# An adaLN transformer block in fp32: the down weights' sums moved to batch 0's projections, and work of gate/up pinned behind PE's reads

## The chip, the cores and the metric
The kernel runs on one core of a Trainium2 chip. The metric is the device time of one execution in microseconds (us). The kernel before took 2990.94 us in the median of 3 runs (2985.1 to 2992.16). One more execution was profiled; all durations below are from it.

Five engines work beside each other, each in its own order: TensorE (PE, matrix products), VectorE (DVE), ScalarE (ACT), GpSimd (POOL) and SyncE (SP), which here issues most DMAs. They meet through semaphores.

## The reference
Two batches of 1024 tokens with D = 1024, 32 heads, a hidden width of 2752 in the feed-forward part, all in fp32:

```python
mod = (_silu(c) @ wmod).reshape(2, 6, 1, -1)         # shifts, scales, gates
h = _layernorm(x) * (1 + ca) + sa
q, k, v = split(clip(h @ Wqkv.T, -8, 8)); q, k = LN(q), LN(k)
x = x + ga * (softmax(causal(q k^T * scale + alibi)) v) @ Wout.T
h = _layernorm(x) * (1 + cb) + sb
out = x + gb * ((silu(h @ Wg.T * ag) * (h @ Wu.T * au)) @ Wd.T * ad)
```

Wg, Wu and Wd are ternary (-1, 0, 1), which the kernel doesn't use.

## The kernel before
**Fast products.** Large products are done by the Strassen-Winograd scheme: a product of 2 x 2 blocks takes seven block products (P1, P2, U2, P5, U3, P53, U6) in place of eight, at the price of sums of blocks. A's operands are A11, A12, A22 and the sums S1 to S4, B's are B11, B21, B22 (B12 only enters sums) and T1 to T4. The gate, up and down products use the scheme twice, one inside the other: seven outer **stages** (`STAGES`), each with seven inner products (`CHAIN`). The outer sums of the weights and of the activations need memory and engines other than PE; much of the kernel's order is about where they go.

**Stages, in order of time.**
1. Modulation vectors, and batch 0's projections (`projections`, from about 47 to 400 us): parts 0, 1 and 2 (q, k, v) of four token pairs j each. Part and pair make a running number n = 4 * part + j. For parts 1 and 2 the operand a of a pair comes back from memory (L930, `a<-hop`); part 0 makes it from tokens. A part's weights wB are loaded by `weights_b` (L806), for batch 0 with sums on DVE and POOL (L814, L816). Between the seven products a list `Todo` of smaller PE work runs (transposes, modulation pieces wm with their own loads at L655). `extra(todo, n)` adds this work for number n. Four pieces of wm are held at a time, so a load waits until PE has used an older piece.
2. Attention over both batches, with batch 1's projections and the out projection woven in by a planner (`together`, `share`). Not touched.
3. The last token pairs: `second_batch` makes, from both batches' halves, the B operands of gate/up (outer sums T1 to T4, then inner sums by `inner_b`, L1161 to L1164, each four subtractions of 128x256 and stores to `bop_dram`). `second(j)` calls it for pair j; the last one, `second(3, nc.vector)`, stands right before gate/up and is all on DVE.
4. Gate/up: five slabs s of 512 hidden columns. For each slab four quarters of both weights are loaded (`gate_weights`), their outer sums made by `gate_sums` (L1615 to L1618, POOL, 128x1024 each), and then come 7 stages n_ with 7 steps each. A step multiplies one inner operand of gate and of up (`sig`, `siu`, or a block of the weights; inner sums at L1626 to L1629 on POOL) by one loaded operand `bt` of 512 KB (`moving`, L1638, six buffers, SP's queue). Each step has two groups of four matmuls, 1.72 us apart: 3.43 us. `merge` (L1565 to L1576) adds a finished bank to the partial results, on DVE or ACT. PE can't write a bank again before its merge has read it.
5. Within gate/up a queue holds side work with due times: `after(n, go)` puts it n steps ahead, and `run_due` emits it. In it are the Silu and the product by up (`final`, L1683 and L1684) and the outer sums of the activations, which are stored to `act_dram` (L1751, L1752). Stage A11 writes X, A12 writes C, S1 writes Z and so on; two more POOL sums stand after S2 and S3 (L1730, L1737).
6. Also within gate/up, one slice of the down weights per stage for the first 20 stages in program order: `down_load` (L1176, two loads of 256 KB, tile wdr), and five steps later `down_weights` (L1184 to L1187, four POOL subtractions of 128x256 into wdo; L1189, four stores of 128 KB to `wdop`).
7. Down: 7 stages of 4 pairs (`products`, L1843 the matmuls, `finish` the output). A stage's weights are loaded in four pieces (`stage_weights`, L1812), T1 to T4 of the inner scheme made at L1813 to L1816; the activations of a pair are one tile aq of 1280 KB (L1823, three buffers). The tiles dsi hold the activations' inner sums (`ais`, three buffers).

**What sets the order.** The program states the work in one order; a scheduler then orders each engine's instructions by priority and by its own idea of when they are ready, unless a dependency or a pin (`behind`, a dependency without a semaphore on the same engine) forbids it. On the chip each engine runs its list strictly in order. SP does the same with DMAs: a store whose source isn't ready holds every load behind it. A memory region is reused when a pool that lies over it is opened, so the first tile there waits for the last reads of the old one.

Of the kernel before, what the change touches and what calls it, by code (L numbers as in the profile page):

```python
# [480 lines left out]
def kernel(  # L481
# [376 lines left out]
    class Todo:  # L858
# [15 lines left out]
        def places(self, q0, n):  # L874

            order = [q for _, _, _, q in SEVEN]

            def between(q):
                if order.index(q) >= q0:
                    yield from self.run(n)  # L880

            return between
# [26 lines left out]
    def projections(b, pools, banks, places, extra=None, other=None):  # L909
# [7 lines left out]
        for part in range(3):  # L917
            bt = weights_b(wp_, wqkv_t[:, ts(part, D)], f"{b}_{part}", wt_dram[part], other, b == 0 and part == 1)
            for j in range(NT // 2):
# [19 lines left out]
                def read(q, bank):  # L939
# [13 lines left out]
                    lambda q, i: a[:, SLOT[q], i, :], bt, banks, read, todo.places(q0, n), KC // 2  # L953
# [202 lines left out]
    def inner_b(o, block, j, pool, eng):  # L1156

        v = block.rearrange("p (q c) h t -> p q c h t", q=2)
        b11, b12, b21, b22 = v[:, 0, :, 0], v[:, 0, :, 1], v[:, 1, :, 0], v[:, 1, :, 1]
        t_ = pool.tile([P, 4, 2, P], FP, tag="inner", name=f"inner_{o}_{j}", bufs=2)  # L1160
        eng.tensor_sub(t_[:, 0], b12, b11)  # L1161
# [6 lines left out]
        nc.sync.dma_start(to[:, 3:7, j], t_)  # L1168

    def down_load(i, pool):  # L1170

        s, c_ = i // 4, i % 4
        w = pool.tile([P, 4, 2, P], FP, tag="wdr", name=f"wdr_{i}")
        rows_ = wd_t[ds(s * 4 * P, 4 * P), :].rearrange("(j p) e -> p j e", p=P)
        for n in range(2):
            nc.sync.dma_start(w[:, :, n], rows_[:, :, ds(n * HALF + c_ * P, P)])  # L1176
        return w

    def down_weights(i, w, pool):

        s, c_ = i // 4, i % 4
        B11, B12, B21, B22 = (w[:, 2 * kh : 2 * kh + 2, n] for kh, n in ((0, 0), (0, 1), (1, 0), (1, 1)))
        ot = pool.tile([P, 4, 2, P], FP, tag="wdo", name=f"wdo_{i}")
        nc.gpsimd.tensor_sub(ot[:, 0], B12, B11)  # L1184
        nc.gpsimd.tensor_sub(ot[:, 1], B22, ot[:, 0])
        nc.gpsimd.tensor_sub(ot[:, 2], B22, B12)
        nc.gpsimd.tensor_sub(ot[:, 3], B21, ot[:, 1])  # L1187
        for r, o in enumerate(("T1", "T2", "T3", "T4")):
            nc.sync.dma_start(wd_dram[o][:, s, :, ts(c_, P)], ot[:, r])  # L1189
# [111 lines left out]
    def second_batch(j, pool, h0, h1, half):  # L1301
# [4 lines left out]
        nc.vector.tensor_sub(t1, lo1, t1)  # L1306
        nc.vector.tensor_sub(t2, hi1, t1)
        half.tensor_sub(t3, hi1, lo1)
        half.tensor_sub(t4, t4, t2)
        for o, v, eng in (  # L1310
            ("T2", t2, nc.vector), ("T1", t1, nc.vector), ("T3", t3, half),
            ("B22", hi1, nc.vector), ("T4", t4, half),
        ):
            inner_b(o, v, j, pool, eng)
# [73 lines left out]
    with ExitStack() as st:  # L1388
# [3 lines left out]
        wosp = st.enter_context(tc.tile_pool(name="wos", bufs=1))  # L1392
        nxp = st.enter_context(tc.tile_pool(name="next", bufs=1))
# [20 lines left out]

        def extra(todo, n):
# [6 lines left out]
            if n == 3:  # L1422
# [13 lines left out]
        dense0 = projections(0, qpools, banks, 2, extra, wxp)  # L1436
# [55 lines left out]
    opools, _, bt, todo, _ = out_args  # L1492
    rest_st = ctx.enter_context(ExitStack())
    rest_pool = right["rest"] = rest_st.enter_context(tc.tile_pool(name="rest", bufs=1, side="right"))
    rps = rest_st.enter_context(tc.tile_pool(name="rest_ps", bufs=4, space=PSUM))

    def fetch(b, j, eng=nc.sync):
        kept[b, j] = rest_pool.tile(
# [7 lines left out]
    def second(j, eng=nc.gpsimd):  # L1506
        second_batch(j, rest_pool, kept[0, j], kept[1, j], eng)
# [51 lines left out]

    def merge(q, bank, to, frm, part_t, pool, nm):  # L1560

        if q in ("P1", "U2", "P5"):
            m, n = {"P1": (0, 0), "U2": (0, 1), "P5": (1, 1)}[q]
            part_t[q] = pool.tile(list(bank.shape), FP, tag=f"{nm[0]}{q}", name=f"{nm}_{q}")
            if frm is None:  # L1565
                nc.scalar.copy(part_t[q], bank)
            else:
                nc.vector.tensor_add(part_t[q], frm(m, n), bank)  # L1568
            return
        m, n = QUAD[q]  # L1570
        if q != "U6":
            nc.vector.tensor_add(to(m, n), part_t[MATE[q]], bank)  # L1572
        elif frm is None:
            nc.scalar.copy(to(m, n), bank)
        else:
            nc.vector.tensor_add(to(m, n), frm(m, n), bank)  # L1576

    with ExitStack() as ff:
# [9 lines left out]
        with ExitStack() as gu:  # L1588
# [23 lines left out]
            def gate_sums(W):  # L1612
                for mat in ("g", "u"):
                    o = W[mat]
# [330 lines left out]
```

## Time and profile before

| | |
|---|---|
| median of 3 runs | 2990.94 us (2985.1 to 2992.16) |
| profiled execution: time, span | 2987.97 us, 2986.3 us |
| mean granted clock of PE | 0.965 |
| PE idle, 0 to 400 us | 36 us (363.90 busy) |
| 400 to 1570 (attention to gate/up's start) | 116 us (1053.90 busy) |
| 1570 to 1762 (gate/up, slab 0) | 42 us (149.87 busy) |
| 1762 to 2472 (gate/up, slabs 1 to 4) | 16 us (693.53 busy) |
| 2472 to 2986 (down) | 35 us (478.52 busy) |
| moved by DMA | 579.12 MB, mean 194 GB/s |

How to read it: the span runs from the first to the last instruction of the profiled execution, the time has a little around it. Busy times of engines overlap. A timeline line has the start, the time, the engine, the source line, the operation, what it writes and reads, and in brackets the idle time before it and what ended it. A line of the waits has the total, the number and the longest. PE's two stretches of waiting on a matmul group are seen against the groups beside them: a group of four 128x512 matmuls takes 1.88 us from first start to last end when PE runs at its full clock.

### The profile page before, as it was taken

To read this page: it belongs to the slowest core of one execution; us is meant where nothing else is said; L and a number is where in the kernel's file an instruction comes from. 1 tells how busy PE (TensorE), PEld (TensorE's weight loads), DVE (VectorE), ACT (ScalarE), POOL (GpSimd) and SP (SyncE) were. 2 spreads that over 40 slices of the span, in tenths; PEclk is the share of its full clock that TensorE was granted. 3 is DMA by queue.
4 is the path that set the end of the run, shared out by engine and by line. 5 is a ranking of instruction groups with operands and counts; after the bars stand their busy time and mean duration, and the time that the engine had idled before them with its cause. 6 is when DMAs were issued, how large, how long until landed. Compare 5 with 4: busy or idle time off the path is not lost. (4 is left out here: it accounts for less than half of the span.)

```text
span 2986.3 us, 29722 instructions
## 1 busy us (share of the span) xinstructions
PE 2739.7 (92%) x10271; PEld 1339.0 (45%) x10271; DVE 1476.0 (49%) x2295; ACT 687.2 (23%) x1523; POOL 1277.0 (43%) x1140
## 2 busy tenths in 40 slices
PE   7999899999998888888997869999999997999998
PEld 2444333333332222224563324444444446888776
DVE  5666424566453456564564333453535354444553
ACT  1322144444434455553111001010101100000000
POOL 3211033334354555564555556564635540222343
PEclk9999999999999899999998989999999998999999
DMA  9777762534535445334777778675766658555542
GB/s 347 278 269 290 273 210 98 186 136 162 182 109 187 140 152 156 115 113 131 226 247 227 240 246 276 187 276 169 270 183 229 197 176 258 159 143 141 152 141 79
DMA packets 376931, 579.12 MB, mean 194 GB/s; under 512 B 20950, under 2 KB 278072, under 8 KB 365636
## 3 DMA queue, kind: packets, MB, share of 16 engines
q1 hardware_dynamic: 366904, 559.78, 57.5%
q10 hardware_dynamic: 9868, 17.35, 1.8%
q8 instruction: 84, 1.38, 0.2%
q14 instruction: 75, 0.61, 0.1%
HBM read 411.89 MB, written 165.17 MB: 193 GB/s over the span
## 5 line engine op out<-in xcount | busy, mean ns | idle before, releaser
L1053 ACT ACTIVATE p<-sc,kw 128x128 f32<-128x128 f32 (+3 forms) x1024 | 422.1, 514 | 335.1 <-PE sc L745 320.2
L1085 POOL TENSOR_TENSOR p<-p,p 128x1024 f32<-128x1024 f32 (+3 forms) x128 | 265.3, 2072 | 255.8 <-PE av L745 227.1
L745 PE MATMUL bank<-wT,a 128*128 128x512 f32 x768 | 361.4, 613 | 13.6 <-DVE wT L814 6.8
L1085 DVE TENSOR_TENSOR p<-p,p 128x1024 f32<-128x1024 f32 (+3 forms) x192 | 248.8, 1309 | 118.1 <-POOL p L1057 69.7
L745 PE MATMUL bank<-wB,a 128*128 128x512 f32 x576 | 265.0, 604 | 2.7 <-DVE raw L947 2.2
L745 PE MATMUL sc<-cq,ck 32*128 32x512 f32 (+3 forms) x1536 | 198.3, 557 | 68.9 <-ACT p L1053 68.5
L1057 POOL TENSOR_SCALAR_AFFINE_SELECT p<-p 128x256 f32<-128x256 f32 x256 | 136.6, 544 | 227.3 <-ACT p L1053 224.4
L745 PEld LDWEIGHTS bank<-wT,a 128*128 128x128 f32 x768 | 141.8, 194 | 200.3 <-issue 177.2
L745 PE MATMUL av<-p,cv 128*32 128x512 f32 (+3 forms) x1536 | 170.5, 513 | 3.9 <-POOL p L1057 3.9
L745 PEld LDWEIGHTS bank<-wB,a 128*128 128x128 f32 x576 | 104.8, 191 | 148.1 <-issue 129.6
L1712 PE MATMUL gx<-bt,sig 128*128 128x512 f32 x280 | 135.4, 607 | 31.6 <-DVE g_P L1568 18.3
L1712 PE MATMUL gy<-bt,sig 128*128 128x512 f32 x280 | 135.3, 606 | 25.6 <-DVE gX L1572 20.6
L745 PEld LDWEIGHTS sc<-cq,ck 32*128 32x128 f32 x1536 | 66.2, 190 | 201.7 <-ACT p L1053 118.5
L1712 PE MATMUL ux<-bt,siu 128*128 128x512 f32 x280 | 134.6, 604 | 2.2 <-DVE u_U L1568 1.1
L1712 PE MATMUL uy<-bt,siu 128*128 128x512 f32 x280 | 132.3, 595 | 0.0
L949 DVE TENSOR_TENSOR raw<-P,bank 128x512 f32<-128x512 f32 x48 | 32.9, 686 | 159.8 <-PE bank L745 157.5
L1712 PEld LDWEIGHTS gx<-bt,sig 128*128 128x128 f32 x280 | 53.3, 192 | 101.4 <-issue 99.7
L1712 PEld LDWEIGHTS gy<-bt,sig 128*128 128x128 f32 x280 | 53.7, 194 | 95.4 <-issue 72.1
L745 PEld LDWEIGHTS av<-p,cv 128*32 128x32 f32 x1536 | 33.3, 110 | 120.9 <-issue 86.8
L1712 PEld LDWEIGHTS ux<-bt,siu 128*128 128x128 f32 x280 | 54.3, 195 | 73.7 <-issue 70.3
L1712 PEld LDWEIGHTS uy<-bt,siu 128*128 128x128 f32 x280 | 53.8, 192 | 68.3 <-issue 67.3
L1712 PE MATMUL gx<-bt,wgS 128*128 128x512 f32 x160 | 75.4, 593 | 2.1 <-DMA bt<-bop_B 1.1
(418 smaller groups left out, 4516.1 us busy)
## 6 DMA issues: line engine op xcount, KB each, us to landing
bt<-bop_T SPq DMA_DIRECT2D x140, 512.0 KB
bt<-bop_B SPq DMA_DIRECT2D x99, 512.0 KB
a<-hop SPq DMA_DIRECT2D x20, 1792.0 KB
wm<-in_L_wmod_dram SPq DMA_DIRECT2D x48, 512.0 KB
wB<-in_L_attn_Wqkv_dram SPq DMA_DIRECT2D x21, 1024.0 KB
aq_S<-act_S SPq DMA_DIRECT2D x16, 1280.0 KB
qk<-qs SPq DMA_DIRECT2D x16, 1024.0 KB
act_S<-asS SPq DMA_DIRECT2D x30, 512.0 KB
```

The source lines that it names most:

```text
L745: return in_order(nc.tensor.matmul(*args, **kw_))
L949: nc.vector.tensor_add(dst, part_t[MATE[q]], bank)
L1053: nc.scalar.activation(p[:, g, lo:hi], sp[:, g, lo:hi], AF.Exp, bias=kw[:, d, h_ : h_ + 1])
L1057: nc.gpsimd.affine_select(out=p[:, :, 0:P], in_=p[:, :, 0:P], pattern=[[0, 2], [1, P]], compare_op=ALU.is_ge, fill=0.0, base=0, channel_mu ...
L1085: adders[b](half, jb).tensor_add(dst, dst, ps[half][:, :, 0:n])
L1712: nc.tensor.matmul(ps.rearrange("p (j t) -> p j t", j=NJ), ins[mat][qa][:, c2, :], bt[:, :, c2, :], start=(q in ("P1", "P2", "P5") and c2 ...
```

## The change
It has five parts.

1. The 20 down-weight slices move from gate/up's stages to batch 0's projections. A function `side(n, e)` is called before each of the seven products e of number n; for n in 1, 2, 3, 5, 6, 7, 9 it emits one slice at each even e, three for each n and two for n = 9, so 9 slices in part 0, 9 in part 1 and 2 in part 2. A slice is now four loads of 128 KB into one tile of five parts, four POOL subtractions in place, four stores. The pool has two buffers. `mod_load` of the first wm pieces starts at n = 2 and not 3.
2. `second(3)` is no longer one block before gate/up: its two outer sums on DVE and the inner sums of T1, T2 and B22 are queued for the steps after 1 to 5, T3 and T4 on POOL for the steps after 8 to 11. The pools of results Z and of activation sums open two stages later, when the pair's pool is closed.
3. `gate_sums` is cut into quarters: 32 POOL operations of 128x256 a slab instead of 8 of 128x1024.
4. In `final` the Silus and the products by up are queued apart, the products one or two steps after the Silus. The activation sums have due times of their own, the last (S4) later than the others. What DVE runs from the queue is pinned: its first instruction stands `behind` the last merge emitted on DVE (`last_read`).
5. Down's pools are opened in another order, so that its weights and aq lie over the gate/up weights' regions; B12 has its place with the T tiles, B22 has one for even and one for odd stages, ais has two buffers instead of three. The first stage's weights and the first two aq are issued on ACT's queue (`nc.scalar`) and not SP's.

The core of the diff:

```diff
+        def side(n, e):
+            at = (1, 2, 3, 5, 6, 7, 9)
+            if n in at and e % 2 == 0 and at.index(n) * 3 + e // 2 < min(4 * NSB, at.index(n) * 3 + 3):
+                down_weights(at.index(n) * 3 + e // 2, dwp)
...
-            if n == 3:
+            if n == 2:
                 loaded.extend(mod_load(wmr, nc.sync, *pieces[i]) for i in range(AHEAD))
...
-        w = pool.tile([P, 4, 2, P], FP, tag="wdr", name=f"wdr_{i}")
+        w = pool.tile([P, 5, 2, P], FP, tag="wdr", name=f"wdr_{i}")
...
+        for kh in range(2):
+            for n in range(2):
+                nc.sync.dma_start(w[:, 2 * kh + n], rows_[:, 2 * kh : 2 * kh + 2, ds(n * HALF + c_ * P, P)])
+        nc.gpsimd.tensor_sub(w[:, 0], w[:, 1], w[:, 0])
+        nc.gpsimd.tensor_sub(w[:, 4], w[:, 3], w[:, 0])
+        nc.gpsimd.tensor_sub(w[:, 1], w[:, 3], w[:, 1])
+        nc.gpsimd.tensor_sub(w[:, 2], w[:, 2], w[:, 4])
+        for o, r in (("T1", 0), ("T2", 4), ("T3", 1), ("T4", 2)):
+            nc.sync.dma_start(wd_dram[o][:, s, :, ts(c_, P)], w[:, r])
...
-            second(3, nc.vector)
...
-                    nc.gpsimd.tensor_add(o["S1"], o["S3"], o["A22"])
...
+                    for k in range(4):
+                        o = {q: v[:, k] for q, v in W[mat].items()}
+                        nc.gpsimd.tensor_add(o["S1"], o["S3"], o["A22"])
...
             def run_due(all_=False):
                 while queue and (all_ or queue[0][0] <= count[0]):
-                    queue.pop(0)[1]()
+                    read = last_read[0]
+                    ins_ = queue.pop(0)[1]()
+                    if ins_ is not None and read is not None:
+                        behind(ins_, read)
+            on_dve, on_pool = second_batch(3, pair_pool, kept[0, 3], kept[1, 3])
+            for e, go in enumerate(on_dve):
+                after(1 + e, go)
+            for e, go in enumerate(on_pool):
+                after(8 + e, lambda go=go: (go(), None)[1])
...
+                    for l in range(2):
+                        after(n, lambda l=l: silu(l))
+                    for l in range(2):
+                        after(n + 1 + l, lambda l=l: product(l))
...
+                            n = 7 + 4 + l if e == 3 else z + 2 + (3 * l + e) // 2
+                            after(n, lambda r=r, l=l: go(*r, l))
...
-                    i = next(slices, None)
-                    if i is not None:
-                        wd_ = down_load(i, dwp)
-                        after(5, lambda i=i, wd_=wd_: down_weights(i, wd_, dwp))
...
+            wdp, aqp, wtp, aip, dpp, dxp, late, drp, fnp, dlp = (
+                dn.enter_context(tc.tile_pool(name=n, bufs=k))
+                for n, k in (
+                    ("wdq", 1), ("aq", 3), ("wdt", 1), ("ais", 2), ("dpart", 2), ("dresx", 1),
+                    ("wdl", 1), ("dres", 1), ("fin", 3), ("drest", 1),
+                )
+            )
...
-                nc.sync.dma_start(
+                (nc.sync if n_ or i > 1 else nc.scalar).dma_start(
                     aq, act_dram[oa][:, :, :, :, ts(i, P)].rearrange("p s l h t -> p (s l) h t")
...
-                wt = stage_weights(STAGES[n_][1])
+                wt = stage_weights(STAGES[n_][1], n_ % 2, nc.sync if n_ else nc.scalar)
```

## The prediction, made before the changed kernel was run
> **What bounds the kernel now.** I read the page's busy times first, then its chain of work that ended last, the waits of the whole core, the timelines of TensorE (PE), VectorE (DVE), GpSimd (POOL) and SyncE (SP) around each wait of PE, and last the windows of 50 us.
>
> ```profile
> PE 2739.7 (92%) x10271; PEld 1339.0 (45%) x10271; DVE 1476.0 (49%) x2295; ACT 687.2 (23%) x1523; POOL 1277.0 (43%) x1140
> PE 37%; POOL 4%; issue 3%; DMA 3%; DVE 2%; SPq 0%; ACT 0%; POOLq 0%; DVEq 0%
> ```
>
> PE is busy for 2739.7 of 2986.3 us and the change takes no matmul away, so it can only win PE's idle time, 247 us in all, or lose more. POOL, DMA and DVE hold small shares of the chain: they matter in a few places.
>
> ```profile
> POOL wdo L1184 <- DMA wdr<-in_L_ffn_Wd_dram: 86.7, 16, 14.0
> DVE uZ L1684 <- POOL uZ L1737: 46.2, 10, 23.7
> ```
>
> The waits (total, times, longest) show POOL, which works in order, standing 86.7 us before down-weight slices, and DVE behind POOL for 23.7 us at once. PE's timeline shows where that reaches PE (start, duration, what, idle before it and its releaser):
>
> ```profile
> 1585.74 3.78 PE L1712 MATMUL gy<-bt,sig 128*128 128x512 f32 x4 [20.57 <-DVE gX L1572]
> 1589.32 2.66 PE L1712 MATMUL uy<-bt,siu 128*128 128x512 f32 x4
> 1591.82 1.88 PE L1712 MATMUL gx<-bt,sig 128*128 128x512 f32 x4
> ```
>
> A group of four takes 1.88 us, yet 3.78 and 2.66 after this idle time: a long gap costs another 2.7 us of slow clock (granted 0.80 in 1550 to 1600). DVE and POOL in that gap:
>
> ```profile
> 1577.92 2.44 DVE L1164 TENSOR_TENSOR inner_T<-oo,inner_T 128x256 f32<-128x256 f32 x1
> 1580.29 0.41 DVE L1161 TENSOR_TENSOR inner_B<-h2t 128x256 f32<-128x256 f32 x1
> ```
>
> ```profile
> 1577.57 2.52 POOL L1618 TENSOR_TENSOR wuS<-wuA,wuS 128x1024 f32<-128x1024 f32 x1
> ```
>
> The same DVE subtraction takes 2.44 us beside a POOL sum of 128x1024 and 0.41 once POOL is done at 1580.1. DVE sits in the last pair's operands while PE waits for a merge. Then slab 0 and its end:
>
> ```profile
> 1703.84 3.49 PE L1712 MATMUL gy<-bt,sig 128*128 128x512 f32 x4 [4.10 <-DMA bt<-bop_B]
> ...
> 1769.97 1.19 PE L1712 MATMUL gx<-bt,sig 128*128 128x512 f32 x1 [18.32 <-DVE g_P L1568]
> ```
>
> ```profile
> 1693.05 5.68 SPq L1189 DMA_DIRECT2D wdop_T<-wdo  x3
> 1698.83 0.42 SPq L1176 DMA_DIRECT2D wdr<-in_L_ffn_Wd_dram  x1
> 1699.30 0.55 SPq L1638 DMA_DIRECT2D bt<-bop_B  x1
> ```
>
> ```profile
> 1763.61 1.73 DVE L1684 SCALAR_TENSOR_TENSOR uZ<-uZ,vt,gZ 128x1024 f32<-128x1024 f32 x1 [23.65 <-POOL uZ L1737]
> ```
>
> SP issues in order: the operand bt stands behind a slice's stores, those behind POOL, POOL behind the slice's load. At the slab's end a product on DVE waits 23.65 us for POOL, and the merges PE needs stand behind it. The last place is down's start:
>
> ```profile
> 2490.28 4.61 PE L1843 MATMUL dx<-wd_B_B,aq_A 128*128 128x256 f32 x10 [15.84 <-issue]
> ```
>
> ```profile
> 2462.96 9.73 SPq L1823 DMA_DIRECT2D aq_A<-act_A  x3
> 2474.89 2.56 SPq L1752 DMA_DIRECT2D act_S<-asS  x1
> ...
> 2484.04 3.49 SPq L1812 DMA_DIRECT2D wd_B_B<-in_L_ffn_Wd_dram  x4
> ```
>
> The waits call it issue, but SP's rows name it: the weights go out at 2484.04, behind stores of sums that DVE has yet to make.
>
> **What the change gains.** Each stall is idle time plus slow groups, less what is late next.
> A, last pair's operands: 20.57 + (3.78 + 2.66 - 2 x 1.88) = 23.3. Their DVE operations, about 12 of 0.42 and 2 of 1.2 = 7.5 us, now lie between merges. T3 and T4 go to POOL behind 32 quarter sums (32 x 0.72 = 23 us from 1559.5), two 128x1024 operations (3.6) and their own four (2.9): T3 is done near 1589, with 2 for sharing with DVE 1591, T4 after eight operand sums and its own four (8.7) near 1600. In the built order SP has T3's store ahead of stage 1's fifth bt and T4's ahead of the sixth. A bt lands some 5 later (a wdr takes 4.9): 1596 and 1605. PE wants the fifth 11 steps of 3.43 after 1554.7, at 1592.4, 4 before it lands, and the sixth then at 1600, 5 before. So 9 takes the old stall's place (0 to 15: POOL early by 9, or late by 6): gain 14 (8 to 23).
> B, slab 0: the idle times before PE's groups from 1677 to 1745 that name bt are 1.14 + 2.40 + 4.10 + 3.45 + 0.19 + 1.89 = 13.2, the slow groups 3.49 and 2.92 add 2.7; with the slices gone SP has no POOL wait among the bt: gain 16 (13 to 18; three short waits on DVE, 2.7 together, are the upper end).
> C, slab 0's end: 18.32 + 2.7 slow = 21. No slice holds POOL, and the products are pinned behind merges one step after Silu; 1.5 left over for the sums of 1.2 among merges: 19.5 (15 to 21).
> D, the other slab ends: idle 2.47 + 0.54, 2.46, 2.46 + 0.54 = 8.5, about 1 left at each: 5.5 (0 to 8).
> E, down's start: 15.84, plus 4.61 + 2.69 for two times ten matmuls that take 2.33 warm (2.6) = 18.5. First weights and two aq leave on ACT's queue, over buffers free before gate/up ends. Only B12 lies over bt buffers and goes out after the last read; PE has P1 and P2 of three pairs first (30 x 0.216 = 6.5 us) against a load of 5 to 6 (a slice's wdr takes 4.9) and two sums of over 1 us each: 5 left (2.5 to 13), gain 13.5 (5 to 16). Fewer ais buffers may cost down up to 10 (PE's waits there for DVE's d_P are 7.1 now); I take 0, because PE runs without a gap between those four waits.
> Together 14 + 16 + 19.5 + 5.5 + 13.5 = 68.5 (41 to 86).
>
> The row here is a DMA share of 1.00 at 314 GB/s in 2450 to 2500, 0.53 in the 50 us before. The Trainium skill (DMA: Bandwidth & Descriptors, "Issuing engines are not separate DMA queues") says that ACT's queue feeds the same 16 engines as SP's, so a second queue brings no bandwidth. If these loads could not leave before 2450, that makes E nothing and the time 13.5 us longer; the share of 0.53 says that there is room earlier.
>
> **What it costs: batch 0's projections.** Per slice four loads, four POOL subtractions of 0.72 and four stores, so 160 DMAs on SP instead of 120, all in order, with two buffers.
>
> ```profile
> 50.00:100.00 50.00, 49.86 (x151) 24.05 (x149) 38.36 (x86) 14.01 (x35) 20.73 (x16) 0.99 0.88 313
> 100.00:150.00 50.00, 46.38 (x139) 22.58 (x139) 33.38 (x71) 15.34 (x36) 15.46 (x13) 0.97 0.68 254
> 150.00:200.00 50.00, 47.95 (x135) 18.85 (x134) 35.70 (x68) 7.14 (x18) 10.59 (x8) 1.00 0.83 306
> ```
>
> (Columns: PE, weight loads, DVE, ACT, POOL, granted clock, DMA share, GB/s.) POOL has room, DMA little, and PE is at its peak: what goes wrong here is paid in full. A slice by before's rows: four issues of 0.47 (1.9), 4.9 from a wdr issue to its first subtraction, 2.9 on POOL, 2.8 for four stores = 12.5; two in flight share the waits, about 16 a pair.
> F, part 0 to 1: by the built program's order nine slices stand on SP ahead of part 1's last two weights, and those ahead of its first operand a. From about 75 us, 4.5 pairs x 16 = 72, and 10 for what else SP issues there: 157, where before issued a at 130.42 and PE took it at 156.61. Weights of 2 x 1 MB and a of 1.8 MB at 306 GB/s need 13: PE starts near 171, 15 late (5 to 30: a pair of 14 to 19). The POOL sums that make each a of batch 0 (L785, L786) also stand behind the slices' subtractions, 2.9 each: PE reaches that a a whole pair of tokens, some 27 us, later. Three wm loads that start a pair earlier, 1.5 MB, lie in the same count of SP's work.
> G, part 1 to 2: nine slices again, and on SP seven pieces wm and two weights now precede a. wm waits for buffers that PE frees at the border: 3.6 + 2.1 + 1.8 MB at 291 to 306 GB/s is 25 us, of which PE fills about 10 with transposes and wm products moved ahead: 15 (0 to 25; nothing where wm's buffers come free earlier). PE's two waits for wm in part 2 (3.32 + 3.98 = 7.3) should then go: -7 (-7 to 0).
> H, DVE beside POOL's 80 subtractions (58 us): PE's waits on DVE's raw are 6.8 + 2.2 = 9.0 now; I take a third more, 3 (0 to 9).
>
> The row is the 2.44 against 0.41 us above. The Trainium skill (SBUF — State Buffer, "SBUF: two separate sides") calls the port that DVE and POOL share an exclusive lock, held for a whole instruction. That favours the quarter sums, but makes each of the 80 a possible stop of DVE in a stage where PE has no idle time: if all reached PE, H would be 58 and the sum near -12 rather than -42. Against it, DVE and POOL together are busy 59.1 of 50 us in the first window with PE at 49.86.
>
> Costs 15 + 15 - 7 + 3 = 26 (-2 to 64). Net 68.5 - 26 = 42.5: 2987.97, the profiled execution's time (1.67 above its span), becomes **2945.5**, against the median of the runs shown, 2990.94, 45 less.
>
> **Rivals.**
> 1. The projections hide the slices: loads land in under 4 us and a arrives in time, as a share of 0.68 to 0.88 may allow. F and G are 0: 2987.97 - 68.5 - 7 + 3 = 2915. Against: SP's order, which no bandwidth mends.
> 2. The gate/up stall and down's start change only their names: bt behind the stores of POOL's T3 and T4, B12 behind the last bt, the DMA still full. A 8, B 14, C 17, D 3, E 5 = 47, less 26: 2967. For: the share of 1.00.
> 3. Slower: SP's order starves both borders. Each us more per pair of slices comes 4.5 times at either border, 9 us together; from 42.5 / 9 = 4.7, a pair of 20.7 instead of 16, nothing is won. At 22 the costs are 26 + 54 = 80: 2999. For: the slices also wait on SP behind hop and wos, whose sources are late (SP stands 5.17 us in one row at 100.33); a full DMA lengthens each landing. Against: in slab 0 POOL began a slice every 10 us (1660.36, 1670.47, 1680.12), beside a bt of 512 KB every 3.43.
> 4. That it does not do what it says: the built order has the slices in the projections and the pins behind their merges, so of this only rival 2 is left.
>
> **How the numbers follow.** About 0.3% (9 us) is what a measurement of this kernel can tell from no change. Forecast (2929 to 2965) 0.46; rival 1 (2905 to 2929) 0.16; rival 2 (2965 to 2979) 0.16; in between, where gains are short and borders dear (2979 to 2997), 0.09; rival 3 (over 2997) 0.13. Faster 0.46 + 0.16 + 0.16 = 0.78, same 0.09, slower 0.13. The range leaves out rival 3, the low end of rival 1 and the last of the case in between: 2912 to 2993.
>
> **What would show it.** A: no DVE row of 2.5 us near 1570, PE's first gap under 15. B: no SP wait on wdo after 1550. C, D: PE gaps at slab ends near 1. E: gap before dx under 8. F, G: PE waiting for a at the first product of parts 1 and 2, some 15 us each; if SP issues part 1's a before 145 us, rival 1; after 175, rival 3. I am wrong if gate/up is no shorter by 45 us, or if PE idles over 70 us more before 400.

## The result, and the profile after
The changed kernel took 2985.14 us in the median of 20 runs (2972.23 to 3016.43), the kernel before 2989.82 in 20 runs (2977.87 to 2995.73). The ratio is 1.0 (0.9978 to 1.0021): no difference that can be measured, where 2945.5 was forecast. Ratios and their intervals use undisturbed runs alone, so in some comparisons below the ratio differs from that of the medians.

The profiled execution of the changed kernel took 2972.97 us (span 2971.2, clock 0.967). That is at the fast end of its own runs: ten of the 20 lie from 2972 to 2982, eight from 2988 to 2998, two above 3009. So two things need a cause: why the profile shows 15 us of gain and not 42, and why the median shows 5.

After's page, busy times and chain:

```profile
PE 2727.8 (92%) x10271; PEld 1341.3 (45%) x10271; DVE 1447.8 (49%) x2285; ACT 684.6 (23%) x1523; POOL 1297.4 (44%) x1270
...
PE 37%; DVE 3%; issue 2%; DMA 2%; POOL 1%; SPq 0%; POOLq 0%; DVEq 0%
```

PE's busy time fell by 12 us, with its mean clock at 0.967 and not 0.965, and POOL's share of the chain from 4% to 1%: the stalls that named POOL are gone. PE's starts at four landmarks tell where the time went:

| us in the span | before | after | difference of the stretch that ends here |
|---|---|---|---|
| first attention product (sc) | 380.13 | 424.19 | +44.1 |
| first gate/up group | 1554.71 | 1593.24 | -5.5 |
| last gate/up group | 2472.56 | 2473.88 | -37.2 |
| end of the span | 2986.3 | 2971.2 | -16.4 |

The projections lost 44 us and everything behind them won 59. After's PE in the projections (lines of the changed kernel: L745 is any product, L748 transposes, L618 the modulation pieces):

```profile
171.58 9.60 PE L745 MATMUL bank<-wB,a 128*128 128x512 f32 x16 [10.56 <-DMA a<-hop]
...
252.43 1.92 PE L618 MATMUL more<-wm,sc 128*32 128x512 f32 x4 [9.35 <-DMA wm<-in_L_wmod_dram]
...
325.11 2.79 PE L748 MATMUL more<-ident,raw 128*128 128x128 f32 x12 [6.67 <-DVE raw L730]
```

Part 1's first product comes at 171.58, where before PE reached it at 156.61. After's SP issued its operand a at 157.03, where before's row has 130.42:

```profile
157.03 0.67 SPq L932 DMA_DIRECT2D a<-hop  x1
```

The second of PE's lines is a modulation piece late by 9.35. The third is new in kind: transposes wait for DVE's normalisation. Before, such waits for DVE's raw and xt came to 2.5 us between 160 and 400; after, to 16.2.

After's PE in gate/up and at down's start (L1768 are gate/up's groups, L1883 down's):

```profile
1631.12 3.43 PE L1768 MATMUL gx<-bt,wgA 128*128 128x512 f32 x4 [15.83 <-DVE gX L1587]
...
1795.89 1.98 PE L1768 MATMUL gy<-bt,sig 128*128 128x512 f32 x4 [3.41 <-DVE gX L1587]
...
2486.82 4.39 PE L1883 MATMUL dx<-wd_B_B,aq_A 128*128 128x256 f32 x10 [6.74 <-DMA aq_A<-act_A]
```

Three old stalls have smaller ones in their places: 20.57 became 15.83, the 18.32 at slab 0's end became 3.41, the 15.84 at down's start 6.74. The line of 1795.89 comes again, with 3.40, at each of the three other slab ends.

**The 15.83.** After's SP, then POOL, then DVE around it (on SP, L1171 and L1172 are stores of the last pair's operands; on POOL, L1315 is an outer sum for T4; on DVE, L1167 is an inner subtraction):

```profile
1626.47 0.36 SPq L1171 DMA_DIRECT2D bop_T<-hl  x1
1626.93 1.01 SPq L1172 DMA_DIRECT2D bop_T<-inner_T  x2
```

```profile
1624.09 2.35 POOL L1315 TENSOR_TENSOR hl<-hl,oo 128x1024 f32<-128x1024 f32 x1
```

```profile
1630.04 0.43 DVE L1167 TENSOR_TENSOR inner_B<-h2t 128x256 f32<-128x256 f32 x1 [17.38 <-DMA bop_T<-inner_T]
```

SP's row before the first one ended at 1608.10. Then it stood for 18.4 us with the store of hl, which POOL finished at 1626.4, behind its 32 quarter sums. The stores of inner_T behind it on SP, whose data were ready, could not go; those inner tiles have two buffers, so DVE could not begin the next one for 17.38 us, and the merges that PE needed stood behind it on DVE.

**The 3.41.** After's DVE at the end of slab 0 (L1587 merges a bank, L1710 are the products of Silu and up, L1728 sums of activations):

```profile
1789.48 0.67 DVE L1587 TENSOR_TENSOR uX<-u_P,uy 128x512 f32<-128x512 f32 x1
1790.07 3.50 DVE L1710 SCALAR_TENSOR_TENSOR uX<-uX,vt,gX 128x1024 f32<-128x1024 f32 x2
1793.50 1.74 DVE L1728 TENSOR_TENSOR asS<-uX,asS 128x1024 f32<-128x1024 f32 x1
1795.16 0.68 DVE L1587 TENSOR_TENSOR gX<-g_P,gy 128x512 f32<-128x512 f32 x1
```

The pin does what it says: the products stand behind the merge of uy, the last that the program emitted. The merge of gy, emitted just before it, isn't named by the pin, and in the built order it stands behind two products and a sum (5.2 us). It is the one that PE waits for, although PE had filled gate's bank first:

```profile
1783.74 1.88 PE L1768 MATMUL gy<-bt,wgA 128*128 128x512 f32 x4
1785.45 1.88 PE L1768 MATMUL uy<-bt,wuA 128*128 128x512 f32 x4
```

### The profile page after: what moved, and what is told of

The parts are those of the page before. It is cut to its first block, busy times and chain, and to the rows that moved or that the text cites. A ratio compares the mean times of both kernels' runs of the same rounds, so it can differ in the third digit from the quotient of the medians.

```text
span 2971.2 us, 29892 instructions
## 1 busy us (share of the span) xinstructions
PE 2727.8 (92%) x10271; PEld 1341.3 (45%) x10271; DVE 1447.8 (49%) x2285; ACT 684.6 (23%) x1523; POOL 1297.4 (44%) x1270
## 5 line engine op out<-in xcount | busy, mean ns | idle before, releaser
L745 PE MATMUL bank<-wT,a 128*128 128x512 f32 x768 | 354.7, 606 | 13.0 <-DVE wT L814 7.2
L745 PE MATMUL bank<-wB,a 128*128 128x512 f32 x576 | 266.5, 608 | 15.4 <-DMA a<-hop 14.7
L745 PE MATMUL sc<-cq,ck 32*128 32x512 f32 (+3 forms) x1536 | 195.8, 553 | 68.3 <-ACT p L1056 68.2
L745 PEld LDWEIGHTS bank<-wT,a 128*128 128x128 f32 x768 | 141.2, 192 | 199.5 <-issue 178.2
L745 PEld LDWEIGHTS bank<-wB,a 128*128 128x128 f32 x576 | 106.1, 193 | 159.4 <-issue 134.2
L745 PE MATMUL av<-p,cv 128*32 128x512 f32 (+3 forms) x1536 | 169.8, 511 | 3.9 <-POOL p L1060 3.9
L745 PEld LDWEIGHTS sc<-cq,ck 32*128 32x128 f32 x1536 | 65.6, 189 | 198.8 <-ACT p L1056 118.5
L1768 PE MATMUL gy<-bt,sig 128*128 128x512 f32 x280 | 136.8, 612 | 14.6 <-DVE gX L1587 14.6
L1768 PE MATMUL gx<-bt,sig 128*128 128x512 f32 x280 | 131.6, 592 | 0.0
L1768 PE MATMUL uy<-bt,siu 128*128 128x512 f32 x280 | 131.6, 592 | 0.0
L1768 PE MATMUL ux<-bt,siu 128*128 128x512 f32 x280 | 131.6, 592 | 0.0
L1768 PEld LDWEIGHTS gy<-bt,sig 128*128 128x128 f32 x280 | 54.2, 196 | 85.1 <-issue 66.3
L745 PEld LDWEIGHTS av<-p,cv 128*32 128x32 f32 x1536 | 33.3, 109 | 120.8 <-issue 87.0
L1768 PEld LDWEIGHTS gx<-bt,sig 128*128 128x128 f32 x280 | 53.6, 192 | 68.1 <-issue 67.6
L1768 PEld LDWEIGHTS ux<-bt,siu 128*128 128x128 f32 x280 | 53.2, 190 | 67.0 <-issue 65.5
L1768 PEld LDWEIGHTS uy<-bt,siu 128*128 128x128 f32 x280 | 53.2, 190 | 67.0 <-issue 65.7
L745 PE MATMUL rest<-hl,restw 128*128 128x256 f32 x288 | 67.2, 391 | 15.7 <-DMA x<-xr 15.7
```

Source lines behind the costliest of these rows:

```text
L745: return in_order(nc.tensor.matmul(*args, **kw_))
L1768: nc.tensor.matmul(ps.rearrange("p (j t) -> p j t", j=NJ), ins[mat][qa][:, c2, :], bt[:, :, c2, :], start=(q in ("P1", "P2", "P5") and c2 ...
```

## The experiments
For the projections three theories were set against each other: **O**, the order on SP (a slice's stores hold the loads behind them); **B**, the bytes; **P**, POOL's subtractions. For gate/up: that the remaining waits are the side work that DVE runs at the slab ends, and theory **L**, that in some executions a sum on DVE comes late beside POOL's long train of quarter sums (seen first in e1). Diffs are against the changed kernel. The experiments ran in four rounds, in which before's median was 2984.76 to 2987.93; a drift of up to 5 us is in every difference to after's median.

**e1, no slices.** `side` emits nothing; down reads raw blocks for T1 to T4.

```diff
-            if n in at and e % 2 == 0 and ...:
+            if False and n in at and e % 2 == 0 and ...:
```

> The changed kernel without the 20 slices: none is loaded, summed or stored, and down's T operands are raw blocks of the down weights in their place (same bytes and descriptors), so the output is not the reference's. It prices the projections' share of the change. Theory O (SP's order and the two buffers delay the operands of parts 1 and 2), theory B (the slices' 20 MB take DMA bandwidth from a stage that has little left) and theory P (POOL's 80 subtractions block DVE) all expect the first attention product at 380 to 388 us instead of 424.2, the time 36 to 44 below the changed kernel, near 2945. If it lies above 2965, the loss is elsewhere.

2958.14 us (2940.2 to 2961.51), ratio 0.9888 (0.9861 to 0.9915). The first attention product is back at 380.49, gate/up starts at 1552.67. So the slices cause the whole loss in the projections, and at gate/up's start cost 40.6 us. The time fell by only 27 in the median, for gate/up took 907.8 us from first to last group and not 880.6. e1's DVE, POOL, SP and PE after slab 0:

```profile
1763.92 11.24 DVE L1726 TENSOR_TENSOR asS<-uX,asS 128x1024 f32<-128x1024 f32 x1
```

```profile
1774.15 1.59 POOL L1643 TENSOR_TENSOR sig<-wgS,sig 128x256 f32<-128x256 f32 x1
```

```profile
1775.19 0.32 SPq L1727 DMA_DIRECT2D act_S<-asS  x1
1775.60 2.79 SPq L1652 DMA_DIRECT2D bt<-bop_B  x5
```

```profile
1780.20 3.75 PE L1766 MATMUL gx<-bt,wgA 128*128 128x512 f32 x4 [10.06 <-DMA bt<-bop_B]
```

A sum on DVE that takes 1.2 to 1.8 us elsewhere in this trace took 11.24. While it lasted POOL ran quarter sums, and then inner sums, of 0.73 without a gap; the one at 1774.15 took 1.59, and within it the sum on DVE ended, at 1775.16. SP stood with the sum's store, five loads of bt behind it, and PE lost 10.06 us and a slow group. A second such sum took 10.99 at 1951.39.

**e2, a quarter of the bytes.** The slices' loads, subtractions and stores cover 32 of 128 partitions; down reads raw blocks. Number and order of all DMAs stay.

```diff
-                nc.sync.dma_start(w[:, 2 * kh + n], rows_[...])
+                nc.sync.dma_start(w[0:32, 2 * kh + n], rows_[0:32, ...])
```

> The changed kernel with every slice cut to 32 of 128 partitions: the same number of loads, subtractions, stores and waits in the same order, a quarter of the bytes (down's T operands are raw blocks again, so the output is not the reference's). O expects little: SP waits for the same POOL operations and buffers; first attention product at 410 to 420. B expects most of the 44 us back: 385 to 395. P expects 424.

**e3, no subtractions.** The four POOL operations of a slice are left out, its loads and stores stay.

> The changed kernel without the slices' 80 POOL subtractions: the loads are stored as they are (all 160 DMAs and all bytes kept; the output is not the reference's). O expects a part back, since a slice's cycle loses its 2.9 us on POOL: first attention product at 400 to 412. B expects none: 420 to 424. P expects nearly all: 382 to 390.

**e4, the slices' stores on POOL's queue.**

```diff
-            nc.sync.dma_start(wd_dram[o][:, s, :, ts(c_, P)], w[:, r])
+            nc.gpsimd.dma_start(wd_dram[o][:, s, :, ts(c_, P)], w[:, r])
```

> The changed kernel with the slices' stores issued by POOL's own queue behind its subtractions, so that SP never waits for POOL there (in the changed kernel it waits 41 us for the slices' subtractions before 425). Bytes and sums are the same. O expects the first attention product at 395 to 408. B expects 420 to 428. P expects 424 or later.

| | median, us | ratio | first attention product | PE's waits from 160 to 400: for a | wm | raw and xt |
|---|---|---|---|---|---|---|
| before | | | 380.1 | 0 | 7.3 | 2.5 |
| after | 2985.14 | 1.0 (0.9978 to 1.0021) | 424.2 | 14.7 | 14.1 | 16.2 |
| e2 | 2989.17 | 0.9997 (0.9977 to 1.0016) | 414.5 | 9.8 | 9.1 | 19.3 |
| e3 | 2995.28 | 1.0029 (1.0006 to 1.0052) | 415.2 | 15.0 | 2.4 | 23.0 |
| e4 | 3009.03 | 1.004 (1.001 to 1.0071) | 428.0 | 0 | 15.3 | 32.6 |

Three quarters of the bytes are worth 10 of the 44 us, the subtractions 9. Both figures are good to some 4 us only: in the profiles whose projections are after's (after, e5, e6, e7, e9, e11, e12, e13) the first attention product lies anywhere from 420.7 to 427.5. O fails as it was stated: with the stores off SP the waits for a are gone (part 1's first a leaves at 145.30 and not at 157.03), so they were SP's order, but attention starts no earlier. The edit has a price of its own: the 80 stores take POOL 0.73 us each, 58.2 in all, so POOL is busy for 197.8 of the first 420 us, where after has 136.8, and the place of the waits for a is taken by waits for DVE's raw (one of 22.07). So e4 shows where the waits for a came from and not what SP's order costs in all. None of the three alone is shown to be the cause. What stays in e2 and e3 is the count and order of the DMAs and PE's order around them, in which transposes were moved ahead of the products whose operands are late. These two were not separated, so for most of the 44 us the cause within the slices stays open.

The times of e3 and e4 are not lower than after's although e3's projections are shorter: their profiles hold late activation sums, one of 11.15 us in e3 and three of 11.0 to 11.3 in e4 (its profile is the second slowest of its 12 executions); e2's holds none.

**e5, whole sums.** POOL's 32 quarter sums a slab become 8 of 128x1024, as before the change.

```diff
-                    for k in range(4):
-                        o = {q: v[:, k] for q, v in W[mat].items()}
+                    o = W[mat]
```

> The changed kernel with gate_sums whole again: 8 POOL operations of 128x1024 per slab in place of 32 of 128x256. Theory L (the spread of the changed kernel's times, 2972 to 3016, comes from DVE's last activation sum of a slab, which in some slabs and some executions takes 11 us in place of 1.6, because POOL's quarter sums follow each other without a gap and DVE does not get its turn; SP's next bt stand behind that sum's store) expects no DVE operation above 4 us in gate/up, no 10 us wait of PE for a bt at stage 1, all times within about 8 us of each other, and a median near the changed kernel's lowest ones, 2968 to 2982. The rival (a late bt is the DMA's or SP's doing, and the quarters help, as the change has it) expects the same two or three clusters of times and a few us more at gate/up's start.

3001.1 us (2998.82 to 3008.38), ratio 1.0054 (1.0038 to 1.007). The median missed, the spread did not: 9.6 us between the ends of six executions, and no activation sum above 3.4 us. One late sum is there all the same, just ahead of the first whole gate sums: an outer sum of the last pair on DVE, beside ten inner sums of 128x256 and one operation of 128x1024 on POOL:

```profile
1592.13 9.80 DVE L1308 TENSOR_TENSOR hl<-h2t,hl 128x1024 f32<-128x1024 f32 x1
```

After's took 1.36 at this place. Twelve of the fifteen experiments' profiles (all but e6, e14 and e15) hold such a sum of 9.7 to 9.8 us here. It costs PE little: e2's profile has it and is at the fast end of its runs. The slab ends are worse in e5. e5's DVE and PE at the end of slab 0:

```profile
1791.85 6.05 DVE L1709 SCALAR_TENSOR_TENSOR uX<-uX,vt,gX 128x1024 f32<-128x1024 f32 x2
```

```profile
1801.83 3.78 PE L1767 MATMUL gy<-bt,sig 128*128 128x512 f32 x4 [7.86 <-DVE gX L1587]
```

The two products take 6.05 and not 3.50, a sum 3.37 and not 1.75, and PE waits 7.86 and not 3.41. So quarter sums buy short slab ends and pay with late sums.

**e6, T3 and T4 ahead of the train.** The last pair's outer sums and T3 and T4 are emitted before the first gate sums.

> The changed kernel with the last pair's two outer sums on DVE and all its POOL work (T3, T4, with their inner sums) stated before slab 0 instead of queued for steps 8 to 11; the inner sums of T1, T2 and B22 stay queued. If PE's 15.8 us wait at gate/up's start comes from SP standing with T4's store, behind which the stores of T1's and T2's inner sums free the tile that DVE needs, it falls to under 6 and the time by 10 to 16. If it comes from DVE or POOL having too much work there, it stays or moves a step.

2986.37 us (2969.79 to 3006.1), ratio 0.9998 (0.9975 to 1.0021); a late sum of 11.22 in its profile. The wait at gate/up's start became 12.74, three steps earlier, where after has its 1.02. So with SP's stand of 18 us gone the next wait is nearly as long: DVE stood for 11.45 us until a store had read one of the two inner tiles, which POOL's T3 and T4 now hold (e15 shows the same).

**e7, sums earlier, products later.** All sums are due two steps after their product in every slab (slabs 0 to 3 had four), the last sum one step later, Silu's products of X one step later.

```diff
-                            n = 7 + 4 + l if e == 3 else z + 2 + (3 * l + e) // 2
+                            n = 7 + 5 + l if e == 3 else z + 2 + (3 * l + e) // 2
-                        z = 4 if s < NSB - 1 else 2
+                        z = 2
-                        final("X", 1, "A12", 1)
+                        final("X", 1, "A12", 2)
```

> The changed kernel with the activation sums due two steps earlier in slabs 0 to 3 (as in slab 4), and the Silu, products and last sums of X one step later. In the changed kernel DVE runs three to four sums, two products and another sum (some 10 us) between the last merges of a slab and the merge of the next slab's second product, and PE waits 3.4 us, with slow groups about 5, at each of four slab ends. If this backlog is the cause, the waits fall to under 1.5 and the time by 10 to 20; the 11 us sums may stay, rarer or not. If the order of PE's uy and gy is the cause, they stay at 3.4.

2957.61 us (2955.15 to 2960.37), ratio 0.9907 (0.9893 to 0.9921): 28 us below after's median with three numbers changed; which of the three did it was not separated. Gate/up from first to last group is 861.6 us, 19 shorter than after's. e7's PE at slab 0's end:

```profile
1794.11 1.10 PE L1768 MATMUL uy<-bt,siu 128*128 128x512 f32 x2 [0.27 <-DMA bt<-bop_B]
```

The waits at the slab ends are gone, no activation sum is late in the profile, and the six times spread by 5 us only. The wait at gate/up's start stays (2.26 + 14.05).

**e8, slices in another place.** They stand beside batch 1's projections, which the planner weaves into attention, two for each pair; their pool is opened earlier.

```diff
+            if e in (0, 3) and 2 * n + e // 3 < 4 * NSB:
+                down_weights(2 * n + e // 3, dwp)
-        dense0 = projections(0, qpools, banks, 2, extra, wxp, side)
+        dense0 = projections(0, qpools, banks, 2, extra, wxp)
-        yield from projections(1, qpools, banks, 1)
+        yield from projections(1, qpools, banks, 1, side=side)
```

> The changed kernel with the 20 slices beside batch 1's projections, which run within attention (two per token pair), instead of batch 0's; same tiles, buffers and queues. If the 44 us of the projections are the price of the place (every queue and PE full), and not of the slices, attention starts at 380 to 384 again, attention grows by under 10 us (POOL has over 200 us of idle time there, DMA a share of 0.49), gate/up starts at 1553 to 1565 and the time falls by 25 to 38. If slices cost the same wherever they stand, gate/up still starts near 1590.

2957.5 us (2949.18 to 2981.1), ratio 0.9919 (0.9892 to 0.9945). The first attention product is at 385.7, gate/up starts at 1569.0: 24 us earlier than after's, 16 later than with no slices at all (e1). The place in batch 0's projections was worth 24 us. Here too one sum was late (12.38 us at 1951.33), after which PE waited 11.43 for bt.

**e9, e7 with T3's and T4's stores on POOL's queue.**

> The kernel of e7 (sums two steps earlier) with the stores of the last pair's T3 and T4, direct blocks and inner sums, issued on POOL's queue instead of SP's. If PE's wait at gate/up's start (14.05 us in e7, 15.83 in the changed kernel) comes from SP standing with T4's store for POOL, with the store behind it that frees DVE's tile, DVE no longer waits 17 us for that tile, PE's wait falls under 4 and the time by 12 to 18 from e7's, to 2940 to 2946. If POOL's or DVE's amount of work is the cause, PE's wait stays over 9.

2963.92 us (2960.9 to 2971.43), ratio 0.9933 (0.9913 to 0.9953): missed, it is no better than e7. With SP free the wait was 16.24, and e9's DVE shows another cause:

```profile
1612.11 18.31 DVE L1309 TENSOR_TENSOR oo<-h2t,hl 128x1024 f32<-128x1024 f32 x1
```

An outer sum on DVE lasted until 1630.42; POOL's train ended at 1629.3. What SP's stand did before, a starved DVE does now.

**e10, e8 and e9 together.**

> The kernel of e9 with the slices beside batch 1's projections, as in e8. If the projections, the slab ends and gate/up's start are separate places, the gains add up: e8 was some 27 below the changed kernel, e7 28, e9 by expectation 12 to 18 more, so 2985 - 27 - 28 - 15 = 2915, between 2908 and 2930. If they hide each other, it stays within 10 us of e9.

2932.52 us (2928.23 to 2948.71), ratio 0.9834 (0.981 to 0.9857). The gains nearly add up: e9 and e8 lie 21 and 28 us below after's median, e10 53. That is just above the stated range, and the wait at gate/up's start is still 16.07; a DVE sum of 18.28 us stands there too.

**e11, no pins.** The diff is `if False:` in place of the condition ahead of `behind`.

> The changed kernel without the pins: the products, sums and last pair's DVE work are queued with the same due times, but not tied behind the last merge. If the pin (behind one merge of two, so that the other merge falls behind two products and a sum) makes the 3.4 us waits at the slab ends, they go and with them the 11 us sums, and the time falls by 10 to 25. If the due times make them (e7 moved those alone), the waits stay, and the products come too early as in the kernel before: the time is the same or up to 30 us longer, with waits of DVE for POOL's uZ or ACT's Silu of 5 us and more.

2981.74 us (2970.27 to 2988.96), ratio 0.9985 (0.9971 to 0.9999). e11's PE at slab 0's end:

```profile
1783.38 1.96 PE L1768 MATMUL gx<-bt,sig 128*128 128x512 f32 x4 [2.44 <-issue]
```

The slab ends have the old wait of 2.44 instead of 3.40, while waits of 3.04, 4.70 and 11.24 at gate/up's start and 8.74 at down's remain. Taken by themselves, the pins change the time by nothing or nearly nothing.

**e12 and e13, e7 with whole sums,** in e12 in all slabs, in e13 in slab 0 alone, where the train delays the last pair's operands.

```diff
-                    for k in range(4):
+                    for k in range(4) if s else [slice(0, 4)]:
```

> The kernel of e7 with gate_sums whole, 8 operations of 128x1024 a slab. This asks what the quarters are worth where DVE has no backlog at the slab end. If the quarters help by letting DVE in more often, whole sums cost 5 to 30 us against e7 (each DVE sum of 128x1024 beside them took 3.3 us in e5 and 1.75 in the changed kernel). If all of their effect ran through the backlog, it is within 5 us of e7, near 2958. In both cases no DVE sum of 11 us is to be seen.

> The kernel of e7 with slab 0's gate sums whole (8 operations of 128x1024) and those of slabs 1 to 4 in quarters. Theory L (DVE's work of the last pair stands still while POOL's train of 32 quarter sums runs, directly or through POOL's T4 and SP behind the train) expects PE's wait at gate/up's start to fall from 14.05 to 6 to 8, as in e12, with no waits at the slab ends, as in e7, and the time 6 to 9 below e7's. If the wait is made by the amount of work alone, which is the same, it stays at 12 or more.

e12: 2969.74 us, ratio 0.9951 (0.9935 to 0.9968); e13: 2952.13 (2947.14 to 2964.74), 0.9877 (0.9857 to 0.9896). In both the waits at gate/up's start are 3.8 + 6.8 in place of e7's 2.26 + 14.05. e12 gives this back at the slab ends (1.34, 1.23, 3.55, 3.57). e13's profiled execution, the 2964.74, holds the longest late activation sum, 16.14 us at 1799.96: e7's due times made late sums rarer, they don't exclude them.

**e14, e13 and e8 together.**

> The kernel of e13 with the slices beside batch 1's projections (e8). By e10 (2932.5 with a wait of 16 at gate/up's start) and e13's expected 6 to 9, theory L expects 2918 to 2930, the fastest so far; the rival 2928 to 2940.

**2923.24 us** (2920.64 to 2928.61), ratio 0.9785 (0.9769 to 0.9801): the fastest here, 62 below after and 65 below before's median in this comparison. Gate/up takes 860.2 us from first to last group; its 245 steps of 3.43 are 840. The time fell where theory L put it, the wait did not: it is 12.50, and not the 6 to 9 expected. e14's PE and DVE at gate/up's start:

```profile
1602.98 3.78 PE L1767 MATMUL gx<-bt,wgA 128*128 128x512 f32 x4 [12.50 <-DVE gX L1586]
```

```profile
1596.00 2.56 DVE L1168 TENSOR_TENSOR inner_T<-oo 128x256 f32<-128x256 f32 x1
1598.48 0.41 DVE L1169 TENSOR_TENSOR inner_T<-oo,inner_T 128x256 f32<-128x256 f32 x1
```

With whole sums beside it a subtraction on DVE takes 2.56 us, six of them in a row here, until the train is over: before's picture again (2.44 and 0.41). SP too stands for 13 us here, with the store of hl, until 1598.30.

**e15, no train beside the last pair.** e7 and e8, with T3 and T4 first and slab 0's gate sums emitted only after stage 0.

> The kernel of e8 with e7's due times, the last pair's T3 and T4 on POOL before slab 0's quarter sums, and these stated after stage 0, so that most of the train of 32 runs behind T3, T4 and DVE's last pair. Theory L expects PE's wait at gate/up's start under 8, and the time within 8 us of e14's. If only the size of the pieces counts, the wait stays at 12 to 16 and the time at e10's 2932.

2929.38 us (2925.19 to 2936.58), ratio 0.9813 (0.9793 to 0.9833). The wait at gate/up's start is 12.73, not under 8. e15's DVE:

```profile
1584.13 1.14 DVE L1166 TENSOR_TENSOR inner_T<-hl 128x256 f32<-128x256 f32 x1 [12.53 <-DMA bop_T<-inner_T]
```

Now the chain of the two inner buffers itself is last: DVE waits until stores have read a tile. A third buffer was not tried. So by the traces this wait has three causes, each of which shows when another is gone: SP behind POOL (after, e14), DVE beside POOL's train (e9, e14), and two buffers (e6, e15). No single edit removed it, and what it costs with all three gone stays open.

## Why the prediction was wrong
Gain and cost were each judged by the right places; the forecast of 42.5 fell to 15 in the profile, above all by G, D and A, and to 5 in the median, most likely by a term that was not in it.

| step | predicted | in after's profile |
|---|---|---|
| A, last pair's operands | 14 | 4.9: 23.3 less 18.4 (waits 1.02 + 15.83, slow 1.6) |
| B, slab 0's bt | 16 | 18.5: all waits for bt gone (15.9 with slow groups), and three short ones for DVE (2.7) |
| C, slab 0's end | 19.5 | 17 |
| D, three other slab ends | 5.5 | -6: 16.5 in place of 10.3, slow groups counted in both |
| E, down's start | 13.5 | 6; another 8 at later waits for DVE's d_P |
| F, part 0 to 1 | -15 | -17: waits 3.96 + 10.56 and slow groups; first product at 171.58, predicted 171 |
| G and H, the rest of the projections | -11 (-15 + 7 - 3) | -27.5: waits of 35.7 in place of 8.1 |

The rows come to 4 of the 15; the rest are small waits that went, 5.5 in attention, 3 in gate/up and 2 in down.

- **F held**, by its own working: 4.5 pairs of slices at 16 us on SP put the issue of a at 157, and it is at 157.03. That it is SP's order is supported by e4, where a leaves 12 us earlier and the waits for a vanish.
- **G failed**, and was the largest miss. It took PE's work moved ahead (transposes, modulation pieces) as a filling of 10 us, and the wait for wm as gone (-7). The runs showed the reverse. Transposes that are moved ahead need DVE's normalisation first (16.2 us of waits), and wm waited 14.1 us and not none; the wait for a at part 2's first product, priced at 15, was 4.12. An operation that fills a gap on one engine had its own releaser, which was not looked up. H's row, DVE held up by POOL's subtractions, is at most part of this: without them (e3) the waits for DVE grew. That PE's order makes these waits is read from after's trace and from e1, where they are gone with the slices; no run kept the slices and changed that order alone.
- **A** had the right picture (T3 and T4 behind 32 quarter sums, bt late by 9) and left out what stands behind a store that waits: SP was held for 18.4 us, and with it the inner tiles. The prediction put T3's store "ahead of stage 1's fifth bt" and reckoned bt alone. Its 3.6 for two POOL operations of 128x1024 was short as well: after's took 2.35 each.
- **D and C**: "about 1 left at each" took it that a product pinned behind a merge stands behind the merge that matters. It stood behind the merge of uy and ahead of that of gy (3.40 and 3.41 us of waits). e7, which puts the sums earlier and the products a step later, took the waits away, and e11 shows that without pins the old ones are back.
- **E** had the wrong wait. It looked for what is left in B12's load; PE waited 6.74 for the second aq. It also took it that the first loads find room before 2450. After's ACT shows them later, in ACT's own order behind a Silu that POOL released:

```profile
2452.11 1.15 ACT L1706 ACTIVATE gZ<-gZ,vt 128x1024 f32<-128x1024 f32 x1 [2.29 <-POOL gZ L1793]
2452.24 1.68 ACTq L1852 DMA_DIRECT2D wd_B_B<-in_L_ffn_Wd_dram  x3
2454.10 12.38 ACTq L1863 DMA_DIRECT2D aq_A<-act_A  x2
```

From 2450 to 2475 after's DMA share is 1.00, in the 25 us before 0.52. So there was room, and the loads came after it: they went from SP's order into ACT's. Whether their buffers were free much earlier is not shown. No run moved them, and PE waits 4.4 to 8.7 us for an aq here in all of them. Fewer ais buffers cost nothing, and 8 us were won where 0 was taken.

- **The late sums** were in no step and no rival. Quarter sums were counted only as a help, since each gives DVE a turn after 0.73 us. About 13 us each (10 of idle time and 3 of slow clock), the late activation sums are the likely cause of the two groups among after's times and of the 12 us between its profile and its median; this is inferred, for the slower executions of after have no profile. What supports it: the eight profiles with quarter trains and the change's due times (after, e1 to e4, e6, e8, e11) hold eight of them, and the length of gate/up follows their number: 881 and 882 us with none (after, e2), 891 to 895 with one (e3, e6, e8), 908 with two (e1), 921 with three (e4). e5 and e12, with whole sums, hold none, and of the six profiles with e7's due times and quarter trains one does (e13).

The Trainium skill (SBUF — State Buffer, "SBUF: two separate sides") says that of a DVE operation with two SBUF inputs and a GpSimd operation, whichever starts first has the shared port for its whole instruction and the other waits. The 2.56 us beside whole sums agree. By that sentence alone a DVE sum beside quarter sums would wait for one of them, 0.73 us; e1's waited for more than a dozen and took 11.24. The page does not say who comes next when GpSimd has the following instruction ready, and the measurement decides.

Of the rivals, 1 was wrong: the projections hide little. Rival 2 (2967: the stalls change their names) is nearest to the profile's 2972.97. SP did stand with T4's store at gate/up's start and the DMA was full at down's; but PE waited there for a merge and an aq, and not for bt and B12, and rival 2 had no picture of the slab ends. Rival 3 had the right stage with the wrong price of a slice: costs of 44.5 and not 80. Of the signs given, "I am wrong if gate/up is no shorter by 45 us" came true, with 37; PE idles 38 us more before 400, and not over 70. One sum beside these has a wrong sign: with H at 58 the terms come to 68.5 - 81, a time 12.5 longer, and not "near -12".

## What to carry to other kernels
Before work is moved into a stage without idle time, follow what its waits let through: e8 gave the same slices a place where PE had slack, and that alone was worth 28 us. A store on an in-order queue is as late as its source, and everything behind it is too; and work moved ahead to fill a gap must be checked for its own producer. A pin should stand behind every read that the next products on PE wait for, and not only behind the one emitted last (read from the trace, not tried), and when a kernel's times fall into two groups, profile more than one execution before the rest is explained.

## What the hardware showed that was not expected
- A DVE sum of two 128x1024 operands, 1.2 us where no POOL operation ran beside it and mostly 1.2 to 1.8 beside quarter sums, took 11 to 16 us in some slabs (9.8 to 18.3 in the last pair) beside 128x256 operations that POOL ran without a gap; it ended when the train was interrupted or over. Beside e5's whole gate sums of 128x1024 the same sum took 1.7 to 3.4 us: many short instructions on POOL held DVE up longer than few long ones. That the port is handed back to POOL is an inference from these times.
- It is not regular: most sums in the same place take 1.74 us or less, and gate/up code of the same kind had none, one or more late ones.
- With a quarter of the bytes in the slices the projections won back 10 of 44 us, give or take 4: most of that loss did not go with the size of the transfers.
